# One tile per round in written order between two layers, self rows by plain transfers, and one bias folded into another

## The chip, the cores and the metric

The kernel runs on one NeuronCore of one Trainium2 chip, as a single program. Five engines each take their own instructions strictly in order: PE (matrix products and transposes), DVE (vector work), ACT (activations, and a queue of transfers of its own), POOL (a general processor that here mostly issues indexed transfers, called gathers) and SP (which only issues transfers). They wait for each other through semaphores. The metric is the device time of one execution in microseconds, the median of several runs; lower is better. Before the change it is 4209.92 us (three runs, 4207.29 to 4214.46).

## The reference, cut to what matters

The program is a stack of four blocks over a graph of 1250 nodes with 512 features. Each block adds a graph network, an attention and a feed-forward part to the residual x. Only the end of block 2 and the attention half of block 3 are touched:

```python
# end of block 2's feed-forward (z = residual + y + sh)
mu = jnp.mean(z, axis=-1, keepdims=True)
var = jnp.mean(jnp.square(z - mu), axis=-1, keepdims=True)
y2 = (z - mu) * jax.lax.rsqrt(var + 1e-05) * ln_g + ln_b
x = x + y2
# block 3
xn = _layernorm(x, axis=-1)
# graph convolution: every node also has an edge to itself, of weight 1
row_f = jnp.concatenate([row, loop]); col_f = jnp.concatenate([col, loop])
norm = dinv[row_f] * ew * dinv[col_f]
h = xn @ W
gnn = segment_sum(h[row_f] * norm[:, None], col_f) + b
# linear attention, phi(t) = elu(t) + 1, 8 heads of 64
q, k, v = split(xn @ w_qkv.T); q = phi(q * 0.125); k = phi(k)
mix = (q @ (k.T @ v)) / (q . sum(k) + 1e-8) @ w_out.T + b_out
x = x + gnn + mix
x = x + ffn3(_layernorm(x))          # 32 experts, 2 per token
```

## The kernel before, in words

Tiles and names. The 1250 nodes are ten tiles of 128 rows (the last has 98). x, z, xn hold all ten in on-chip memory; xnT is xn transposed. A product of one tile with a 512x512 matrix is `nat` (L196): four matmuls of 128x512, which the profile shows as eight records.

The end of block 2, called the tail here. `layer2_ffn` leaves four functions per tile in `self.tail` (L3252). `fetch` (L3229) issues two gathers on POOL, of the tile's two expert outputs; six buffers of the tile `g` rotate. `add_rows` (L3234) adds them to z (two DVE instructions, L3237) and takes z's mean and inverse deviation: bn_stats, bn_aggr and an add on DVE (L245 to L247), logarithm and exponential on ACT (L248, L249). `scale` (L3241) makes a bias on DVE (L3242), normalizes on ACT (L3245) and multiplies by gamma on POOL (L3246). `add` adds z to x on DVE (L214) and takes the statistics of x.

`tail_steps` (L2723) chains these four, then `norm` (L2726: xn, on DVE, L262) and `turn` (L2729: four transposes on PE, L2732, and a copy on ACT, L2734). It staggers them over rounds: in the round of tile t each later function works on a later tile. Before, `add` and `norm` of one tile are one step (`arrive`), so a tile passes five steps. `layer3_attn` calls the round of tile t with `need(t)`. In round 0, `load` also asks for the three attention matrices of 1 MB each, on SP, each behind a tiny fill on POOL (L169) that holds the load until then.

The first product of block 3. After each `need(t)` the tile is multiplied with the convolution's matrix (`nat`, L200), scaled on ACT into `o` (L3300) and written to the table gcn_h in device memory from ACT's queue (L3301). All gathers of block 3 read gcn_h, so the first of them waits for the tenth write.

The stage after it. The edges lie in 188 tiles of 128, 16 to a block of 107 target nodes (12 blocks, the last of 12 tiles). In each full block the sixteenth tile holds only the self edges: its 128 places are four runs of 32, of which 27 (26 in the last) are used. For an edge tile, `fetch` (L3317) gathers 128 rows of gcn_h into `hs` (POOL, L271; eight buffers, asked for six tiles ahead), `split` (L3322) makes a high part on ACT (L3326), a low part (L3327) and a one-hot matrix (L3330) on DVE, and PE adds two matmuls into the block's sum (L3366). At a block's end DVE scales and adds a bias (L3373), ACT's queue writes the block, and `add` (L3336) later reads finished rows back from SP (L3338) and adds them to x. Between groups of four edge tiles one step of the attention runs (`next(steps)`): the generator `linear_attention_steps` (L904) has ten steps of k products, ten that add up k and v (L950), one that makes the combined matrix, and then the q products and outputs. For each tile's output it first adds the attention's bias row to x on POOL (L979).

What sets the order. A scheduler orders each engine's instructions from the traced program by its own estimates, and may put an instruction of a later step ahead of one of an earlier step, as long as no data dependence forbids it. In the rounds of the tail only POOL keeps its text order before the change (L2747). `written_order` (L148) is a helper that chains all instructions traced inside it, engine by engine, so that each of the five engines keeps the text's order. Between the edge stage and the experts of block 3 SP also loads expert matrices (L3406) in the same queue as the read-backs.

Of the kernel before, what the change touches and what calls it, by code (L numbers as in the profile page):

```python
# [12 lines left out]
F32 = mybir.dt.float32  # L13
# [7 lines left out]
AF = mybir.ActivationFunctionType  # L21
ALU = mybir.AluOpType
# [3 lines left out]
D = 512  # L26
NT = 10
# [8 lines left out]
BN = 107  # L36
NB = 12
CB = 8
GE = 4
# [10 lines left out]
QN = 27  # L50
QK = 3
QC = 2 * QK
QP = 32
# [13 lines left out]
class Net:  # L67
# [79 lines left out]
    @contextmanager  # L147
    def written_order(self):  # L148

        traced = self.nc.cur_bb.bb.instructions  # L150
        last = traced[-1]
        yield
        at = next(k for k in reversed(range(len(traced))) if traced[k] is last) + 1
        queues = {e: None for e in (mybir.EngineType.PE, mybir.EngineType.DVE,
                                    mybir.EngineType.Activation, mybir.EngineType.Pool,
                                    mybir.EngineType.SP)}
        how = mybir.DependencyInfo(mybir.DependencyClass.NoSync, mybir.DependencyReason.DATA)
        for i in traced[at:]:
            if i.engine in queues:
                if queues[i.engine] is not None:  # L160
                    self.tc.add_manual_dep(i, queues[i.engine].name, how,
                                           reason="written_order")
                queues[i.engine] = i

    def weight(self, src, k, n, behind=False):

# [737 lines left out]
    def linear_attention_steps(self, xn, xT, w_qkv, w_out, b_out, qscale, finish, added=None,  # L904
                               need=None, ws=None):
# [4 lines left out]
        nc = self.nc  # L910
# [9 lines left out]
        with self.tc.tile_pool(name="la", bufs=1) as p, \  # L920
# [3 lines left out]
                wv = self.weight(w_qkv[:, 2 * D:3 * D], 4, D)  # L924
            else:
                wk, wv, wq = ws
            bo = self.rowvec(b_out)

            P = p.tile([128, 4, D], F32, name="P")
            ks = p.tile([128, D], F32, name="ks")  # L930
            for half in range(2):
# [12 lines left out]
                for c in range(5):  # L944
                    m = self.mm()
                    for i in range(HT):
                        t = half * HT + i
                        r = rows(t)
# [3 lines left out]
                    o = P[:, c, :] if c < 4 else ks  # L952
# [23 lines left out]
            for i in range(NT + 2):  # L976
                if i < NT:
                    r = rows(i)
                    nc.gpsimd.tensor_tensor(self.x[:r, i, :], self.x[:r, i, :], bo[:r],  # L979
                                            op=ALU.add)  # L980
                    q = tmp.tile([128, D], F32, tag="q", name="q")
                    phi(q, self.nat(xT, wq, i))
                    prod = tmp.tile([128, D], F32, tag="r", name="prod")
                    nc.vector.tensor_tensor(prod, q, ks, op=ALU.mult)
                    den = tmp.tile([128, 8], F32, tag="den", name="den")
                    nc.vector.tensor_reduce(den, prod.rearrange("p (h d) -> p h d", h=8), AX.X,
                                            ALU.add)
                    finish(den, den)
                    nc.vector.reciprocal(den, den)
                    q8 = q.rearrange("p (h d) -> p h d", h=8)  # L990
                    nc.vector.tensor_tensor(q8, q8, den.unsqueeze(2).to_broadcast([128, 8, 64]),
                                            op=ALU.mult)
                    Q[i] = q
                if 1 <= i <= NT:
                    qT = tmp.tile([128, 4, 128], F32, tag="qT", name="qT")
                    self.transpose_tile(qT, Q.pop(i - 1))
                    QT[i - 1] = qT
                yield
                if i >= 2:
                    t = i - 2  # L1000
                    self.add_to_x(t, self.nat(QT.pop(t), kvo, 0))
                    if added is not None:
                        added(t)
                    yield
# [1715 lines left out]
        self.tails = ExitStack()  # L2720
        return self.tails.enter_context(self.tc.tile_pool(name=name, bufs=1, side="right"))

    def tail_steps(self, xn, xnT, behind=None):  # L2723


        def norm(t):  # L2726
# [9 lines left out]
        tail = self.tail  # L2736
# [3 lines left out]
            last[0](t)  # L2740
            norm(t)

        steps = tail[:-1] + [arrive, turn]
        n = len(steps) - 1

        def need(t):
# [266 lines left out]
    def layer2_ffn(self):  # L3013
        nc, I = self.nc, self.I
        keep = self.begin_tail("l2t")
        self.begin_convs()
        with self.tc.tile_pool(name="l2f", bufs=1) as p:
            z = keep.tile([128, NT, D], F32, name="z")
            ga = keep.tile([128, D], F32, name="ga")
# [3 lines left out]
            with ExitStack() as es:  # L3023
# [48 lines left out]
                with self.tc.tile_pool(name="l2x", bufs=1) as px:  # L3072
# [3 lines left out]
                    for t in range(NT):  # L3076
                        self.norm_tile(t, z[:, t, :])
                        q = self.tp([128, 4, 128])
# [4 lines left out]
                        for i, (a, b, op) in enumerate(((0, 2, ALU.subtract), (0, 1, ALU.add),  # L3083
                                                        (1, 0, ALU.subtract))):
                            q = t * 128
# [137 lines left out]
            self.convs.close()  # L3223
        self.act_tables()
        mv = keep.tile([128, NT, 2], F32, name="mv")
        rs = keep.tile([128, NT, 2], F32, name="rs")
        pg = self.tails.enter_context(self.tc.tile_pool(name="l2g", bufs=6, side="right"))
        gs = {}

# [9 lines left out]
            self.row_stats(z[:, t, :], mv[:, t, :], rs[:, t, 0:1])  # L3239

        def scale(t):  # L3241
            nc.vector.scalar_tensor_tensor(rs[:, t, 1:2], mv[:, t, 0:1], -1.0, rs[:, t, 0:1],  # L3242
                                           op0=ALU.mult, op1=ALU.mult)
            c = z[:, t, :]
            nc.scalar.activation(c, c, AF.Identity, scale=rs[:, t, 0:1], bias=rs[:, t, 1:2])  # L3245
            nc.gpsimd.tensor_tensor(c, c, ga, op=ALU.mult)  # L3246

        def add(t):
            self.add_to_x(t, z[:, t, :])
            self.ready(t)  # L3250

        self.tail = [fetch, add_rows, scale, add]  # L3252
# [25 lines left out]
    def layer3_attn(self):  # L3278
        nc, I = self.nc, self.I
        added = self.both_added()  # L3280
        with self.tc.tile_pool(name="l3", bufs=1) as p:
# [4 lines left out]
            def load():  # L3286
                ws.extend(self.weight(I["L3_mix_w_qkvT"][:, i:i + D], 4, D, behind=True)
                          for i in (D, 2 * D, 0))

            need = self.tail_steps(xn, xnT, load)  # L3290
            th = self.dram.tile([NP, D], F32, name="gcn_h")
            H = self.dram.tile([NP, D], F32, name="gcn_sum")
            dinv = self.dinv
            w = self.weight(I["L3_gnn_W"], 4, D)
            keep = self.tails.enter_context(
                self.tc.tile_pool(name="gcn0", bufs=2, side="right"))
            for t in range(NT):
                need(t)
                o = keep.tile([128, D], F32, tag="o", name="o")
                nc.scalar.activation(o, self.nat(xnT, w, t), AF.Copy, scale=dinv[:, t:t + 1])  # L3300
                nc.scalar.dma_start(th[t * 128:(t + 1) * 128, :], o)  # L3301
            self.tails.close()
            with self.tc.tile_pool(name="gcn", bufs=2) as tmp:
                if self.fast:
                    dinvb = self.dinvb
                    bias = self.rowvec(I["L3_gnn_b"])
                else:
                    acc = tmp.tile([128, D], F32, tag="acc", name="acc", bufs=3)
                    nc.vector.memset(acc, 0.0)
                steps = self.linear_attention_steps(  # L3310
                    xn, xnT, I["L3_mix_w_qkvT"], I["L3_mix_w_outT"], I["L3_mix_b_out"], 0.125,
                    lambda o, d: nc.vector.tensor_scalar(o, d, 1e-8, None, op0=ALU.add),
                    added, ws=ws)

# [1 line left out]

                def fetch(t):  # L3317
                    hs = tmp.tile([128, D], F32, tag="hs", name="hs", bufs=8)
                    self.gather(hs, th[:, :], self.srcI[:, t:t + 1])
                    W[t] = hs  # L3320

                def split(t):  # L3322
# [21 lines left out]

                tiles = list(range(NT))
                T = self.groups * GE
                for t in range(6):
                    fetch(t)
                split(0)
                for g in range(self.groups):  # L3350
                    next(steps, None)
                    k = g % 4
                    last = not self.fast or k == 3 or g + 1 == self.groups
                    if not self.fast:
# [289 lines left out]
```

## Time and profile before

| what | value |
|---|---|
| median of three runs | 4209.92 us (4207.29 to 4214.46) |
| the profiled execution | 4223.65 us, of which the span of the trace is 4221.9 us |
| granted TensorE clock, mean | 0.939 |
| busy: PE, DVE, ACT, POOL | 87%, 60%, 33%, 29% |
| last expert output of block 2 written | 3481.41 us |
| first product of the tail starts / last table write issued | 3504.87 / 3564.22 us |
| first and last gather of the edge stage | 3571.04 / 3853.46 us |
| last block's bias and scale (L3373) | 3860.42 us |
| experts of block 3 and the end | 3887 to 4222 us |

How to read it. A window row gives, for one stretch of the span, each engine's busy time and number of instructions, then the granted clock of PE (1.00 is full), the share of the sixteen transfer engines that was busy, and GB/s. A wait row says which engine's line waited for whom: total us, times, longest. In the timeline a row is start, duration, engine, line and what it reads and writes; in square brackets stands the idle time before it and what ended it.

### The profile page before, as it was taken

What the parts mean: (1) busy time and instruction counts of PE and PEld (TensorE: products, weight loads), DVE (VectorE), ACT (ScalarE), POOL (GpSimd) and SP (SyncE); (2) the same over time, 40 slices, a digit from 0 to 9 for tenths busy, and PEclk for the clock granted to TensorE, in tenths of its full rate; (3) what the DMA queues carried; (4) which work ended last, traced back from release to release, by engine and by line L of the source; (5) the groups of instructions that cost most, each with busy time, mean ns of one, the idle gap of its engine ahead of it and who ended that gap; (6) DMA issues with size and microseconds to landing.
All of it is one profiled execution on the core that took longest, in us unless ns stands there. A gap on an engine that the chain in (4) does not pass through costs nothing. (4 is left out here: it accounts for less than half of the span.)

```text
span 4221.9 us, 48964 instructions
## 1 busy us (share of the span) xinstructions
PE 3680.2 (87%) x15172; PEld 2163.7 (51%) x15190; DVE 2546.1 (60%) x6105; ACT 1400.3 (33%) x2960; POOL 1204.3 (29%) x1229
## 2 busy tenths in 40 slices
PE   4996998899887669989999999979979986996898
PEld 2443443344333254447888776545456652554465
DVE  7556995885886835248966685142763335796311
ACT  2111332332224832105644462122532323553111
POOL 1007654663761030020000002030311015774422
PEclk9998999999998889999999999999989998996799
DMA  5718886985984154043211113660014654765796
GB/s 186 262 31 249 252 234 203 264 256 170 276 234 140 37 169 138 0 116 108 77 39 52 37 31 120 239 229 19 16 43 153 216 171 144 206 200 195 240 307 172
DMA packets 315682, 657.51 MB, mean 156 GB/s; under 512 B 78797, under 2 KB 128569, under 8 KB 300005
## 3 DMA queue, kind: packets, MB, share of 16 engines
q1 hardware_dynamic: 204909, 386.38, 28.5%
q0 software_dynamic: 73936, 227.19, 19.5%
q10 hardware_dynamic: 36568, 40.73, 2.8%
q8 instruction: 124, 2.03, 0.2%
q14 instruction: 145, 1.19, 0.1%
HBM read 532.93 MB, written 126.53 MB: 156 GB/s over the span
## 5 line engine op out<-in xcount | busy, mean ns | idle before, releaser
L271 POOL DMA_INDIRECT xl<-xl,srcI x531 | 547.5, 1031 | 347.3 <-issue 121.2
L1530 PE MATMUL mm<-hl,oh 118*128 118x512 f32 x564 | 341.3, 622 | 66.9 <-DVE s L1543 32.2
L2475 PE MATMUL more<-hh,e 128*128 128x259 f32 x1600 | 383.7, 385 | 9.2 <-ACT o L2418 8.2
L2475 PEld LDWEIGHTS more<-hh,e 128*128 128x128 f32 x1600 | 295.1, 191 | 72.2 <-issue 16.0
L200 PE MATMUL mm<-w,xnT 128*128 128x512 f32 x640 | 304.2, 615 | 15.0 <-ACT xnT L2734 12.9
L1533 PE MATMUL mm<-xl,ident 128*128 128x512 f32 x524 | 285.2, 626 | 21.6 <-DMA xl<-xl,srcI 21.4
L271 POOL DMA_INDIRECT hs<-gcn_h,srcI x188 | 213.8, 1137 | 81.7 <-issue 25.0
L1543 DVE TENSOR_TENSOR s<-xl,mm 128x512 f32<-128x512 f32 x302 | 205.8, 681 | 28.3 <-PE mm L1530 19.9
L1640 PE MATMUL more<-xl,wT 128*32 128x512 f32 x1698 | 212.7, 609 | 4.2 <-ACT wT L1621 4.2
L1530 PEld LDWEIGHTS mm<-hl,oh 118*128 118x128 f32 x564 | 107.0, 196 | 212.7 <-DVE s L1543 69.7
L1546 DVE SCALAR_TENSOR_TENSOR junk<-s,att 128x512 f32<-128x512 f32 x302 | 209.4, 693 | 10.6
L1546 DVE SCALAR_TENSOR_TENSOR junk<-mm,att 128x512 f32<-128x512 f32 x262 | 180.2, 688 | 57.4 <-PE mm L1533 46.3
L2395 ACT ACTIVATE e<-r,hh 128x512 f32<-128x512 f32 (+1 forms) x240 | 154.3, 646 | 137.2 <-PE more L2475 126.3
L200 PEld LDWEIGHTS mm<-w,xnT 128*128 128x128 f32 x640 | 122.1, 197 | 142.4 <-issue 118.2
L1506 ACT CAST oh<-nb 108x512 fp32r<-108x512 uint8 x141 | 86.8, 617 | 306.7 <-DMA nb<-nbt 292.0
L3366 PE MATMUL more<-hl,oh 128*128 128x512 f32 x376 | 152.9, 512 | 26.0 <-DVE oh L3330 11.3
L2398 ACT ACTIVATE e<-r,a 128x512 f32<-128x512 f32 (+1 forms) x240 | 152.4, 646 | 67.2 <-DVE e L2400 55.0
L2400 DVE TENSOR_TENSOR e<-e,e 128x512 f32<-128x512 f32 (+1 forms) x240 | 141.9, 597 | 50.9 <-ACT e L2395 46.8
L2338 PE MATMUL mm<-w,xnT 128*128 128x258 f32 x640 | 159.7, 392 | 7.4 <-DVE junk L2322 6.0
L881 PE MATMUL more<-ohs,ohb 128*128 128x512 bf16 (+1 forms) x546 | 132.6, 375 | 35.4 <-ACT ohs L865 14.8
L3326 ACT ACTIVATE hl<-hs,rec 128x512 fp32r<-128x512 f32 x188 | 130.7, 718 | 98.1 <-PE more L3366 52.1
L3327 DVE SCALAR_TENSOR_TENSOR hl<-hs,rec,hl 128x512 fp32r<-128x512 f32 x188 | 142.7, 771 | 24.9 <-ACT hl L3326 24.0
(674 smaller groups left out, 7273.6 us busy)
## 6 DMA issues: line engine op xcount, KB each, us to landing
w<-L_ffn_Wp SPq DMA_DIRECT2D x64, 1024.0 KB
w<-L_ffn_table SPq DMA_DIRECT2D x56, 1025.0 KB
neg<-ntab SPq DMA_DIRECT2D x80, 320.0 KB
hl<-xr SPq DMA_DIRECT2D x216, 108.0 KB
xr<-tro SPq DMA_DIRECT2D x30, 512.0 KB
xe<-routed_in SPq DMA_DIRECT2D x56, 256.0 KB
routed_out<-o ACTq DMA_DIRECT2D x56, 256.0 KB
c<-x SPq DMA_DIRECT2D x141, 64.0 KB
```

The lines of the kernel that those rows point to most:

```text
L200: self.nc.tensor.matmul(p, lhsT=xT[:, c, t * 128:(t + 1) * 128], rhs=w[:, c, n0:n0 + n], start=c == 0, stop=c == k - 1)
L271: self.nc.gpsimd.indirect_dma_start(out=out, out_offset=None, in_=table, in_offset=bass.IndirectOffsetOnAxis(ap=idx, axis=0), bounds_check ...
L1530: nc.tensor.matmul(m, lhsT=s, rhs=rows_pair(b, pair)[:K], start=not last, stop=not on_pe(i))
L1533: nc.tensor.matmul(m, lhsT=self.ident, rhs=d["xl"][:, j, :D], start=False, stop=True)
L1543: nc.vector.tensor_tensor(o, d["xl"][:, j, :D], s, op=ALU.add)
L1546: nc.vector.scalar_tensor_tensor(junk, s, 0.0, L["att"], op0=ALU.max, op1=ALU.mult, accum_out=B[g // 4]["lg"][:, i % 16:i % 16 + 1])
L1640: nc.tensor.matmul(d["y"][ps], lhsT=d["w", i][:, ps], rhs=rows_of(t), start=i == 0, stop=False)
L2338: nc.tensor.matmul(m, lhsT=chunk(layer, c)[:, t * 128:(t + 1) * 128], rhs=w[:, c, :], start=c == 0, stop=c == k - 1)
L2395: nc.scalar.activation(e1[:, :n], R[q, k, 0][:, :n], AF.Exp, bias=HH[q][:, s, 256:257])
L2398: nc.scalar.activation(e2[:, :n], R[q, k, 1][:, :n], AF.Exp, bias=heads[q][0][:, s, 0:1])
L2475: nc.tensor.matmul(ys[j], lhsT=e[:, j * 128:(j + 1) * 128], rhs=HH[q][:, s, :], start=s == 0, stop=s == NT - 1)
L3366: nc.tensor.matmul(y, lhsT=oh, rhs=hl[:, i], start=i + j == 0 and not (self.fast and k), stop=last and i + j == GE)
```

## The change

It has three parts. In the tail, `scale` becomes one DVE instruction, (z - mean) * gamma, and the inverse deviation is applied where z is added to x (`add_scaled`, one DVE instruction); the ACT and POOL passes and the small DVE bias are gone. `arrive` is split into `add` and `norm`, so a tile passes six steps, and the whole loop over `need`, product and table write is put into `written_order`, with the table write of tile t - 1 placed between the round of tile t and its product. For the first twelve groups of the edge stage, everything traced on PE, DVE and ACT is ordered behind the last instruction of that engine that was traced before the stage.

In the edge stage, the sixteenth tile of the blocks 0 to 10 is fetched by four plain transfers of 32 consecutive rows each from SP instead of one gather on POOL (eleven tiles of 188).

The attention's bias row is added once to the convolution's bias row on DVE, and the ten additions of it to x on POOL are gone.

```diff
+    def last_of(self, engine):
+        return next(i for i in reversed(self.nc.cur_bb.bb.instructions) if i.engine == engine)
+
+    def after(self, first, others):
+        how = mybir.DependencyInfo(mybir.DependencyClass.NoSync, mybir.DependencyReason.DATA)
+        for i in others:
+            if i.engine == first.engine:
+                self.tc.add_manual_dep(i, first.name, how, reason="after")
...
-            bo = self.rowvec(b_out)
+            bo = None if b_out is None else self.rowvec(b_out)
...
-                    nc.gpsimd.tensor_tensor(self.x[:r, i, :], self.x[:r, i, :], bo[:r],
-                                            op=ALU.add)
+                    if bo is not None:
+                        nc.gpsimd.tensor_tensor(self.x[:r, i, :], self.x[:r, i, :], bo[:r],
+                                                op=ALU.add)
...
-    def tail_steps(self, xn, xnT, behind=None):
+    def tail_steps(self, xn, xnT, behind=None, apart=False):
...
-        steps = tail[:-1] + [arrive, turn]
+        steps = tail + [norm, turn] if apart else tail[:-1] + [arrive, turn]
...
         def scale(t):
-            nc.vector.scalar_tensor_tensor(rs[:, t, 1:2], mv[:, t, 0:1], -1.0, rs[:, t, 0:1],
-                                           op0=ALU.mult, op1=ALU.mult)
             c = z[:, t, :]
-            nc.scalar.activation(c, c, AF.Identity, scale=rs[:, t, 0:1], bias=rs[:, t, 1:2])
-            nc.gpsimd.tensor_tensor(c, c, ga, op=ALU.mult)
+            nc.vector.scalar_tensor_tensor(c, c, mv[:, t, 0:1], ga, op0=ALU.subtract,
+                                           op1=ALU.mult)
 
         def add(t):
-            self.add_to_x(t, z[:, t, :])
+            self.add_scaled(t, z[:, t, :], rs[:, t, :])
             self.ready(t)
...
-            need = self.tail_steps(xn, xnT, load)
+            need = self.tail_steps(xn, xnT, load, True)
...
-            for t in range(NT):
-                need(t)
-                o = keep.tile([128, D], F32, tag="o", name="o")
-                nc.scalar.activation(o, self.nat(xnT, w, t), AF.Copy, scale=dinv[:, t:t + 1])
-                nc.scalar.dma_start(th[t * 128:(t + 1) * 128, :], o)
+            with self.written_order():
+                def put(t, y):
+                    o = keep.tile([128, D], F32, tag="o", name="o")
+                    nc.scalar.activation(o, y, AF.Copy, scale=dinv[:, t:t + 1])
+                    nc.scalar.dma_start(th[t * 128:(t + 1) * 128, :], o)
+
+                y = None
+                for t in range(NT):
+                    need(t)
+                    if y is not None:
+                        put(t - 1, y)
+                    y = self.nat(xnT, w, t)
+                put(NT - 1, y)
...
+                    mixed = self.rowvec(I["L3_mix_b_out"])
+                    nc.vector.tensor_tensor(bias, bias, mixed, op=ALU.add)
...
-                    self.gather(hs, th[:, :], self.srcI[:, t:t + 1])
+                    b, k = divmod(t, 4 * GE)
+                    if self.fast and k == 4 * GE - 1 and b < NB - 1:
+                        for q in range(4):
+                            r = b * BN + QN * q
+                            nc.sync.dma_start(hs[QP * q:QP * q + QP, :], th[r:r + QP, :])
+                    else:
+                        self.gather(hs, th[:, :], self.srcI[:, t:t + 1])
...
+                traced = nc.cur_bb.bb.instructions
+                ahead = [self.last_of(e) for e in (mybir.EngineType.PE, mybir.EngineType.DVE,
+                                                   mybir.EngineType.Activation)]
+                n0 = len(traced)
                 for t in range(6):
                     fetch(t)
                 split(0)
                 for g in range(self.groups):
                     next(steps, None)
+                    if g < 12:
+                        for i in ahead:
+                            self.after(i, traced[n0:])
+                        n0 = len(traced)
```

More of the change, by code (lines that the diff above doesn't have):

```diff
@@ L3225, in layer2_ffn @@
         mv = keep.tile([128, NT, 2], F32, name="mv")
-        rs = keep.tile([128, NT, 2], F32, name="rs")
+        rs = keep.tile([128, NT, 1], F32, name="rs")
         pg = self.tails.enter_context(self.tc.tile_pool(name="l2g", bufs=6, side="right"))
@@ L3310, in layer3_attn @@
                 steps = self.linear_attention_steps(
-                    xn, xnT, I["L3_mix_w_qkvT"], I["L3_mix_w_outT"], I["L3_mix_b_out"], 0.125,
+                    xn, xnT, I["L3_mix_w_qkvT"], I["L3_mix_w_outT"],
+                    None if self.fast else I["L3_mix_b_out"], 0.125,
                     lambda o, d: nc.vector.tensor_scalar(o, d, 1e-8, None, op0=ALU.add),
```

## The prediction

> **What bounds the kernel now.** I read the page's costliest groups first, then windows over the touched stretch, then the waits of its parts, then the timeline between the last products of the tail and the first gather.
>
> The windows (stretch, then busy us and instructions of PE, weight loads, DVE, ACT, POOL, then granted clock, transfer share, GB/s):
>
> ```profile
> 3481.00:3503.00 22.00, 0.00 (x0) 0.00 (x0) 11.09 (x30) 5.03 (x12) 12.59 (x11) 0.58 0.37 109
> 3503.00:3571.00 68.00, 53.01 (x136) 24.18 (x136) 38.69 (x86) 24.26 (x62) 29.82 (x28) 0.91 0.43 147
> 3571.00:3600.00 29.00, 21.97 (x57) 11.32 (x58) 19.33 (x38) 16.91 (x26) 22.56 (x22) 0.88 0.67 186
> 3600.00:3800.00 200.00, 196.74 (x616) 107.88 (x615) 174.21 (x371) 110.56 (x182) 155.03 (x135) 1.00 0.70 203
> 3800.00:3862.00 62.00, 45.09 (x114) 21.44 (x112) 50.00 (x111) 29.24 (x45) 42.94 (x40) 0.81 0.67 203
> ```
>
> Three regimes are to be seen: a tail (3481 to 3571) in which no engine is full; a middle (3600 to 3800) in which PE is busy 196.7 of 200 us; and an end (from 3800) in which PE idles 17 us of 62. The page's row of the gathers (busy us, mean ns, idle before them):
>
> ```profile
> L271 POOL DMA_INDIRECT hs<-gcn_h,srcI x188 | 213.8, 1137 | 81.7 <-issue 25.0
> ```
>
> And the longest wait from 3800 to 3862 (total us, times, longest):
>
> ```profile
> ACT hl L3326 <- DMA hs<-gcn_h,srcI: 17.9, 18, 3.2
> ```
>
> From 3620 to 3800 that same wait is 6.0 us in 5 times; in the end it is 17.9 us. The end is paced by gathers: POOL issues them back to back, 1.0 us and more each plus 0.3 between, and its waits there are nearly all that 0.3.
>
> The timeline of the tail's last tile:
>
> ```profile
> 3550.31 0.55 DVE L262 TENSOR_SCALAR xn<-x,mvx,rsx 128x512 f32<-128x512 f32 x1 [0.50 <-ACT rsx L249]
> ...
> 3558.35 0.60 PE L2732 MATMUL tp<-ident,xn 128*128 128x128 f32 x4
> ...
> 3559.14 0.58 ACT L2734 COPY xnT<-tp 128x512 f32<-128x512 f32 x1
> ...
> 3559.77 10.57 PE L200 MATMUL mm<-w,xnT 128*128 128x512 f32 x24 [0.82 <-ACT xnT L2734]
> ...
> 3564.22 0.33 ACTq L3301 DMA_DIRECT2D gcn_h<-o  x1
> ```
>
> DVE has normalized the last tile at 3550.9, but its transposes stand behind two other products and start at 3558.35. The 24 records are tile 9's product and two k products of the attention. The last table write leaves at 3564.22, the first gather starts 6.8 us later, at 3571.04.
>
> **The change: the order.** In the built programs everything before the tail stands in the same order, but for the new addition of the two bias rows; from the first edge tile on, PE, DVE and ACT keep their orders instruction for instruction. So holding the attention's first steps back changes nothing after the tail, and within it PE still does ten first products and then two k products. New are the order in the tail and the queues of POOL and SP.
>
> **The change: the tail.** What counts is when the last write leaves (3564.22 before). ACT loses ten L3245 (0.81 us), POOL ten L3246 (1.33 us) and five L979 (1.27 us); DVE loses ten tiny L3242, and gains ten passes of 0.75 us (as L3237). In text order a round's vector work for one tile, from start to start in dependent order, is 2 x 0.78 (L3237) + 0.72 + 0.22 + 0.06 (statistics) + 0.67 (scale) + 0.78 (add) + 1.00 (statistics) + 0.47 (norm) = 5.5 us. PE's round is 0.79 (transposes to copy) + 0.63 (copy to product) + 3.56 (eight records of 0.445) = 5.0 us. Round 0 must first run five `add_rows`, four `scale`, three `add`, two `norm`. With the landings seen before (3488.27, then about 1.4 apart) the last of these `add`s ends at 3510.5; ACT's copy stands behind its statistics, so the first product starts at 3511.8, 7 us later than before (3504.87). It takes 5.5 us, as before. Then come 5.5 us rounds while `add_rows` lasts, and 5.0 us rounds: product 9 starts at 3559.0, and the write leaves at 3563.4. With DVE 6% slower it is 3566.2, with 12% 3569; if product 1 is also slow (6.23 us before, at a clock of 0.53) 3565.4. I take 3564.8, nearer the clean rows since POOL's passes, which stretched L3237 to 2.11 us, are gone: **+0.6 us**, ends -0.8 and +5. POOL's twenty gathers of the tail (1.14 us each) stay ahead of DVE: the ninth and tenth are asked for by 3498 and used from 3506. The three attention weights are asked for after twelve gathers instead of ten, at about 3498.5 instead of 3506.1, still long before the k products. The wait of ACT's activation of wq (1.91 us, L936) moves behind the last write and lies in the 5.96 us in which ACT waited for that write. The bias addition (0.69 us, DVE) lies in the experts, where DVE waits for PE over 1 us at a time; if it doesn't, +0.7.
>
> **The change: self rows and bias on POOL.** POOL loses 11 of 188 gathers and five L979 in the edge stage (1.28 us each). Worth by regime:
> At the start tile t's gather is 1.31 us behind its forerunner; without tile 15's the later ones come 1.3 us earlier, and ACT waits for them (11.8 us from 3575 to 3620): **-1.3**.
> In the middle POOL isn't the limit: its gain only builds up a lead. Two L979 (3710.19 and 3747.10) fall where DVE is 95 to 100% busy; the L3327 beside the first took 1.62 instead of 0.75: 2 x 0.9 = **-1.8**, ends 0 and -2.6.
> At the end POOL's lead decides. Counting back from the last gather (tile 187, 3853.46), POOL issues tile 162 at 3817.59, when DVE splits tile 158 (3817.94). Eight buffers allow 166. In the middle POOL saves 9 x 1.44 + 4 x 1.44 = 19 us, so it will stand at that limit: four tiles. Tile 175 is a plain transfer: a fifth. 25 intervals take 35.87 us, 1.435 each: 5 x 1.435 = **-7.2**. DVE would allow more: 28 tiles at 0.87 and 5.9 us of other passes end at 3848, 11 us before tile 187's pair, so DVE isn't reached. Ends: 0 (transfers, not POOL, pace it) and -11.
>
> SP now issues 44 transfers of 64 KB more, in order with the read-backs and expert loads. No row shows such a transfer; 0.35 us an issue makes 1.4 us a tile, and landing as the gathers' (3.5 to 4.7 us from issue). The tightest is tile 159: behind the read-back at 3806.43, it would land at 3812.4, and ACT takes the tile near 3816.6. Slack 4 us: 0 taken, upper end +4 at each of blocks 9 and 10.
>
> Past the last block (3860.42) nothing differs: routing and experts move along.
>
> At this point the Trainium skill speaks against the change ("DMA: Bandwidth & Descriptors", Issuing engines are not separate DMA queues): all queues run on the same sixteen engines, so a second issuer saves only issue time. By that alone the -7.2 would be 0 if the engines paced the end. The rows: transfer share 0.67 there, but 1.04 at 401 GB/s from 3515 to 3520, and POOL issuing without a pause; issue time is the thing short here.
>
> **Sum.** +0.6 - 1.3 - 1.8 - 7.2 = -9.7 us. The profiled execution took 4223.65 (span 4221.9 and 1.75 around it), 13.7 above the median of 4209.92; a fresh one would take 4213.9, and the median 4200.2: 0.23% less.
>
> **Rivals.**
> *Transfers pace the end.* For: 4.2 to 4.7 us from issue to ACT at the end against 3.5 at the start. Against: the share of 0.67. Then only +0.6 - 3.1: 4207.4.
> *POOL paces every block.* For: sixteen gathers at 1.137 + 0.34 are 23.6 us, and blocks take 22.5 to 25.0 (one 30.8). Against: PE 196.7 of 200. Then 11 x 1.48 + 5 x 1.44 = 23.5 goes: 4187.
> *The one-tile rounds leave PE cold, and it is slower.* PE pauses twice in each round. If the clock stays near 0.5, each product takes 6.23 instead of 3.56 us: nine times 2.67 is 24, against the 10.3 won: 4224. It decides where pauses are as long as the 5.07 us ahead of product 1. Against: from 3525 to 3560 PE was busy 28.4 of 35 us, with pauses up to 2.1, at clock 1.00; the rounds now have 4.16 of 5.5 and pauses of 1.3. The Trainium skill ("TensorE: Matmul & The Clock Gate", The HAM clock gate) needs an idle window of about 3.4 us for the slow clock; by it this rival falls.
> *SP brings self rows late.* Each late one holds ACT, and with it PE; 4 us at two blocks: 4208. Against: the slack above.
>
> **How the numbers follow.** Mine 0.46, transfers 0.19, every block 0.18, cold 0.08, SP 0.09. The measurement tells about 0.2%, 8.4 us: faster means under 4201.5, slower over 4218.3. Mine alone reaches from 4195 to 4206, and 0.65 of it is faster: 0.30, with every block 0.48, and 0.01 of the rest. Slower: cold, and 0.01 more. The range takes in 4188 (all 22 us of PE's idle time after the first 5 are won) and 4212 (tail +5, only -3.1 won). Cases of both signs hold most of the chance, so mine stands beside it: 4195 to 4206.
>
> **What would show it.** Right: first product near 3512, rounds of 5 to 5.5 us at clock 1.00, last write within 3 us of 3564; blocks up to the eighth as long as before within 1 us; ACT's wait for hs after 3800 well under 10 us; last block's bias about 10 us earlier against the same start. Wrong: products of 6 us; PE idle before the sixteenth tiles; SP's read-backs behind a self row; an end that still advances 1.4 us a tile with POOL idle.

## The result and the profile after

The changed kernel takes 4191.1 us (median of five, 4185.3 to 4194.0) against 4210.8 (five, 4207.3 to 4220.6) for the kernel before: a ratio of 0.9948, interval 0.9934 to 0.9962. That is faster by 0.52%, or 19.7 us; I had forecast 4200, 9.7 us less. Direction and range held, the size is twice the forecast, and the measured time lies below the 4195 to 4206 that I had given for my own mechanism alone. The first question is whether the other 10 us belong to the change.

The profiled execution of after took 4188.4 us (span 4186.2). Its windows over the answering stretches (us, then busy us and instructions of PE, weight loads, DVE, ACT, POOL, then granted clock, transfer share, GB/s):

```profile
3465.00:3487.00 22.00, 0.00 (x0) 0.00 (x0) 14.41 (x32) 3.31 (x11) 14.87 (x16) 0.58 0.52 146
3487.00:3553.00 66.00, 50.77 (x136) 23.43 (x136) 39.25 (x84) 20.20 (x53) 10.11 (x7) 0.91 0.39 139
3553.00:3582.00 29.00, 21.12 (x57) 10.76 (x57) 18.81 (x37) 16.55 (x26) 22.46 (x22) 0.94 0.67 188
3582.00:3778.00 196.00, 195.91 (x617) 108.12 (x616) 169.25 (x372) 109.72 (x182) 142.81 (x125) 1.00 0.71 210
3778.00:3836.50 58.50, 44.73 (x112) 22.09 (x111) 49.44 (x110) 29.28 (x45) 40.85 (x34) 0.74 0.67 206
```

The tail is no fuller than before. In the middle PE is now busy 195.9 of 196 us: the 3.3 us that it idled there are gone. The end is shorter, but PE still idles 14 us in it, now at a mean clock of 0.74 instead of 0.81. POOL has 11 gathers fewer, each no faster (page, costliest groups):

```profile
L282 POOL DMA_INDIRECT hs<-gcn_h,srcI x177 | 205.8, 1163 | 118.3 <-ACT r L927 48.7
```

The waits of the end, from 3778 to 3837 (total us, times, longest), against 17.9 and 4.6 us before:

```profile
ACT hl L3353 <- DMA hs<-gcn_h,srcI: 11.4, 11, 2.0
...
ACT hl L3353 <- PE more L3401: 10.0, 11, 1.8
```

The tail's last tile, in the timeline of after:

```profile
3529.06 0.55 DVE L273 TENSOR_SCALAR xn<-x,mvx,rsx 128x512 f32<-128x512 f32 x1 [1.60 <-ACT rsx L260]
...
3540.81 0.60 PE L2744 MATMUL tp<-ident,xn 128*128 128x128 f32 x4
3541.45 0.58 ACT L2746 COPY xnT<-tp 128x512 f32<-128x512 f32 x1 [3.64 <-PE tp L2744]
...
3542.08 10.57 PE L211 MATMUL mm<-w,xnT 128*128 128x512 f32 x24 [0.68 <-ACT xnT L2746]
...
3546.54 0.33 ACTq L3311 DMA_DIRECT2D gcn_h<-o  x1
...
3553.14 1.00 POOL L282 DMA_INDIRECT hs<-gcn_h,srcI  x1 [48.70 <-ACT r L927]
```

The last tile waits 11 us for PE, the last write leaves at 3546.54, and POOL, without work for 48.7 us, gathers first at 3553.14.

These clock times are all earlier than before, but not by the change alone: the load of the first product's weight, which SP asks for ahead of the tail, left at 3476.07 before and at 3459.79 after. The profiled execution of before (4223.65 us) lies 13 us above its median, that of after 3 us below its own. So the two executions are compared by stretches, cut at the same instruction in both (starts in the timelines, us; "router" runs from the last block's bias to the first routed write):

| stretch | before | after | difference | forecast |
|---|---|---|---|---|
| start of the kernel to that weight load | 3476.1 | 3459.8 | -16.3 | 0 |
| to the last table write | 88.15 | 86.75 | -1.4 | +0.6 |
| to the first gather | 6.82 | 6.60 | -0.2 | 0 |
| to block 0's bias | 27.14 | 27.42 | +0.3 | -1.3 |
| to block 8's bias | 200.00 | 195.60 | -4.4 | -1.8 |
| to block 11's bias | 62.24 | 59.21 | -3.0 | -7.2 |
| router | 46.65 | 39.73 | -6.9 | 0 |
| experts, to the end | 314.80 | 311.09 | -3.7 | 0 |

What the change touches gives -8.7 us, near my -9.7, made up of other terms. The other 27 us lie in code in which PE, DVE, ACT, POOL and SP keep their orders (but for one DVE addition). The experiments ask which of them come back.

### The profile page after: what moved, and what is told of

Its sections match the earlier page's. It is cut to its first block, busy times and chain, and to the rows that moved or that the text cites. A ratio compares the mean times of both kernels' runs of the same rounds, so it can differ in the third digit from the quotient of the medians.

```text
span 4186.2 us, 48993 instructions
## 1 busy us (share of the span) xinstructions
PE 3667.5 (88%) x15172; PEld 2155.6 (51%) x15190; DVE 2544.6 (61%) x6106; ACT 1393.6 (33%) x2950; POOL 1172.6 (28%) x1198
## 5 line engine op out<-in xcount | busy, mean ns | idle before, releaser
L211 PE MATMUL mm<-w,xnT 128*128 128x512 f32 x640 | 301.3, 609 | 15.8 <-ACT xnT L2746 13.7
L282 POOL DMA_INDIRECT hs<-gcn_h,srcI x177 | 205.8, 1163 | 118.3 <-ACT r L927 48.7
L1518 ACT CAST oh<-nb 108x512 fp32r<-108x512 uint8 x141 | 86.9, 618 | 324.4 <-DMA nb<-nbt 302.4
L3600 DVE TENSOR_SCALAR o<-mm,d 98x512 f32<-98x512 f32 x32 | 24.0, 750 | 216.2 <-PE mm L3597 102.2
```

The source lines that it names most:

```text
L211: self.nc.tensor.matmul(p, lhsT=xT[:, c, t * 128:(t + 1) * 128], rhs=w[:, c, n0:n0 + n], start=c == 0, stop=c == k - 1)
L282: self.nc.gpsimd.indirect_dma_start(out=out, out_offset=None, in_=table, in_offset=bass.IndirectOffsetOnAxis(ap=idx, axis=0), bounds_check ...
```

## Experiment 1: both kernels once more, and the change in three parts

The runs from here on were made in three later series, each beside the kernel before. In the first two, layer 0's edge layers are some 160 to 260 us slower (median of before: 4473 and 4406 us) and single times of before spread over 46 to 71 us. Whether the chip makes this difference is not shown: the first and the third of them ran on a chip of the same number, 10, and before took 4473 us in one and 4405 us in the other. So medians are compared within one series only, and the stretches behind layer 0 across series with care. First both kernels again, unchanged.

> The kernel before, once more, for a second trace. In the first two traces the stretch from the last block's bias to the first routed write took 46.65 us before and 39.73 us after, with the same instructions: the granted clock was 0.50 through the router's products before, and rose to 1.00 in the middle of them after. If that state belongs to the kernel, this trace shows 46.5 to 46.8 us and clock 0.50 from the last block to the first routed write again. If it is chance (the clock changes in steps of 3.41 us, wherever these fall), it may be anywhere from 38 to 47 us here. The 16 us by which the trace of before was late already ahead of the tail should not come back: tail's first write near 3460, time near 4210.

> The changed kernel once more, for a second trace and as the base of the next three. If the plain transfers carry the gain and nothing else is systematic, the parts of the trace are as in the first one: last table write 86.7 us after the load of the first product's weight is asked for, last three blocks 59.2 us (62.2 to 62.8 without plain transfers), and the routing either 39.8 or 46.7 to 47.3 us by chance. Time: 9 us under before by the sum of these parts, 20 us under it if what the first comparison showed beyond them is real.

The totals of another series tell nothing of the 16 us ahead of the tail. But the router took 39.81 us in the kernel before, and 47.25 in the changed one: each other's length of the first pair. The windows of the router in the first traces of before and after:

```profile
3860.50:3907.00 46.50, 27.35 (x124) 25.04 (x124) 26.07 (x71) 4.11 (x10) 0.00 (x0) 0.53 0.42 168
```

```profile
3835.40:3875.00 39.60, 20.59 (x124) 18.34 (x124) 26.19 (x69) 4.10 (x10) 0.00 (x0) 0.63 0.50 198
```

And in the second traces of before and after:

```profile
4129.40:4169.10 39.70, 20.56 (x124) 18.34 (x124) 26.23 (x70) 4.10 (x10) 0.00 (x0) 0.63 0.50 197
```

```profile
4047.40:4094.50 47.10, 28.45 (x124) 26.12 (x124) 26.18 (x69) 4.11 (x10) 0.00 (x0) 0.50 0.42 166
```

The same 124 products take 20.6 us where the clock rises on the way and 27.4 to 28.5 where it does not. So the 6.9 us of the first pair are chance, not the change. Among the ten traces here whose router stands in this order, four are short (39.7 to 39.8) and six long (46.7 to 47.3).

Then the parts. The tail alone, which is the changed kernel with these lines back as before:

```diff
-                    b, k = divmod(t, 4 * GE)
-                    if self.fast and k == 4 * GE - 1 and b < NB - 1:
...
-                    else:
-                        self.gather(hs, th[:, :], self.srcI[:, t:t + 1])
+                    self.gather(hs, th[:, :], self.srcI[:, t:t + 1])
...
-                    mixed = self.rowvec(I["L3_mix_b_out"])
-                    nc.vector.tensor_tensor(bias, bias, mixed, op=ALU.add)
...
-                    xn, xnT, I["L3_mix_w_qkvT"], I["L3_mix_w_outT"],
-                    None if self.fast else I["L3_mix_b_out"], 0.125,
+                    xn, xnT, I["L3_mix_w_qkvT"], I["L3_mix_w_outT"], I["L3_mix_b_out"], 0.125,
```

> Before, with the tail of the change alone (written order, one tile per round, the new scale, the first steps held back); all 188 gathers, and the second bias on POOL. My sum: +0.6 us, time within 2 us of before (4211). If the tail itself were the gain, -10 us or more. By the two traces -1.5 us from the last table write on. The first product 7 us later than in before against the same first landing, rounds 4.8 us without transfers at the end; blocks and end as in before.

The plain transfers alone (the kernel before, with these lines):

```diff
+                    b, k = divmod(t, 4 * GE)
+                    if self.fast and k == 4 * GE - 1 and b < NB - 1:
+                        for q in range(4):
+                            r = b * BN + QN * q
+                            nc.sync.dma_start(hs[QP * q:QP * q + QP, :], th[r:r + QP, :])
+                    else:
+                        self.gather(hs, th[:, :], self.srcI[:, t:t + 1])
-                    self.gather(hs, th[:, :], self.srcI[:, t:t + 1])
```

> Before, with the plain transfers of eleven own tiles alone. My sum: -8.5 us (start -1.3, end -7.2): 4202. By the traces, the edge stage from first gather to last block bias was 289.4 us before and 282.2 after; if the plain transfers carry it, it is 282 to 284 here and the time 4204 to 4206. If the routing's clock belongs to how the end is left, another -6.8 us: 4197 to 4199. If transfers pace the end, 4207 or more.

The bias alone:

```diff
-            bo = self.rowvec(b_out)
+            bo = None if b_out is None else self.rowvec(b_out)
...
+                    if bo is not None:
+                        nc.gpsimd.tensor_tensor(self.x[:r, i, :], self.x[:r, i, :], bo[:r],
+                                                op=ALU.add)
...
+                    mixed = self.rowvec(I["L3_mix_b_out"])
+                    nc.vector.tensor_tensor(bias, bias, mixed, op=ALU.add)
...
+                    None if self.fast else I["L3_mix_b_out"], 0.125,
```

> Before, with the two bias rows added once (ten POOL additions go, one DVE addition comes). My sum: -1.8 us (two additions beside a full DVE), 4209. If POOL's additions cost nothing, 4211. If POOL paced every block, ten additions of 1.28 us plus 0.16 each: -14 us. In the trace: the two blocks with passes of hl stretched to 1.62 us become 0.9 us shorter each, the others unchanged.

Ratios to the kernel before, with intervals, and stretches (us; weight load to last write, first gather to block 0's bias, and on from there):

| kernel | ratio | to last write | to block 0 | to block 8 | to block 11 | router | experts |
|---|---|---|---|---|---|---|---|
| before again | - | 88.22 | 33.83 | 203.44 | 62.84 | 39.81 | 316.62 |
| tail alone | 0.9997 (0.9968 to 1.0026) | 87.90 | 33.35 | 209.09 | 62.81 | 47.27 | 315.51 |
| plain transfers alone | 0.9954 (0.9933 to 0.9976) | 88.12 | 31.30 | 200.76 | 59.82 | 47.33 | 311.99 |
| bias alone | 0.9978 (0.9953 to 1.0002) | 85.70 | 33.89 | 205.62 | 63.99 | 39.82 | 312.86 |
| after again (its own series) | 0.9956 (0.9928 to 0.9984) | 86.81 | 32.74 | 196.07 | 60.46 | 47.25 | 309.33 |

The plain transfers carry it: the only part whose interval leaves out 1, and the end falls by 3.0 us, exactly as in the whole change. The edge stage takes 291.9 us with them against 300.1 in the kernel before of the same series, 8.2 less; the 282 to 284 us that I expected were not met, as the stage is longer in both kernels here. The tail alone changes the total by -1.0 us, within its interval. Its own stretch is 0.3 us shorter than before (87.90 against 88.22), with passes of `add_rows` stretched beside a bias addition that POOL still makes there (timeline of the tail alone):

```profile
3784.17 2.43 DVE L3249 SCALAR_TENSOR_TENSOR z<-g,ev,z 128x512 f32<-128x512 f32 x2
...
3784.35 1.71 POOL L991 TENSOR_TENSOR x<-x,b 128x512 f32<-128x512 f32 x1 [12.45 <-DVE xn L273]
```

The six pairs of these passes before it take 1.53 to 1.54 us.

The bias gives its price where I had looked for it: the two blocks with stretched passes go from 33.73 and 25.64 to 29.87 and 24.35 us here, and from 30.78 and 25.64 to 29.88 and 24.46 in the first pair, 2.1 us together there (forecast 1.8). In its trace other blocks, which I had expected unchanged, were longer (block 1 by 2.2, block 3 by 3.8 us), so that its total, -10 us with 0 inside the interval, can't be read from that one execution.

## Experiment 2: layer 0's edge layers left out

To rid the totals of layer 0's spread, four kernels were run without its three edge layers, so that what they compute differs from the program; from layer 1 on, the first three have the orders of the full kernels.

```diff
-            for k in range(3):
-                otab = self.dram.tile([NP, D], F32, name="x%d" % (k + 1))
...
+            for t in range(NT):
+                self.ready(t)
```

> The kernel before without layer 0's three edge layers (they are left out, x goes on without them). From layer 1 on the order is that of before on every engine. In the traces so far the same code of these layers took from 250 us less to 16 us less in one execution than in another, and the rest of the program repeated within a few us; without them the spread of single times should fall from 30 to 70 us to under 15 us, and the medians of this and the next three can be compared with each other to about 3 us. Their ratio to the full kernel before says nothing.

> The changed kernel, cut in the same way. Against the short kernel before: my sum says -9.7 us; the parts of the traces say -8.6 us (tail -1.4, edge stage -7.2), or -12 to -13 if the 4 us by which the experts were shorter wherever plain transfers were used belong to the change; if the medians of the full kernels (-19.7 and -16 us) are right, -16 to -20. Routing's two lengths (39.8 and 47 us) are chance in all of these theories and spread single times by 7 us.

> The kernel before with the plain transfers alone, cut in the same way. My sum: -8.5 us against the short kernel before, 1.2 us behind the changed one. By the traces -6 to -8 us (blocks to the eighth -2.7, last three -3.0, start 0 to -2.5), so the tail and the bias together are worth 1.5 to 4 us more in the changed one. If the full kernels' -19.6 is right, -16 to -20, and the same as the changed kernel.

Medians (range), us: before 3213.3 (3207.7 to 3229.3), changed 3201.9 (3190.7 to 3207.1), plain transfers alone 3203.6 (3200.8 to 3212.2). The spread fell to 11 to 22 us, not under 15 for all; the router's two lengths can make 7 of it. The changed kernel is 11.3 us faster by the medians, and no time of one lies among those of the other; the plain transfers alone give 9.7. The medians are near my sums (9.7 and 8.5). But the means differ by 17.3 us (3216.5 and 3199.2) and by 12.0 for the transfers alone, so that five to seven times that spread by 11 to 22 us can't tell 10 us from 20. One profiled execution of each in this series, which was one of the slowest of before (3229.0) and the fastest of the changed kernel (3190.7):

| stretch | before | transfers alone | changed |
|---|---|---|---|
| to last write | 88.00 | 88.07 | 86.59 |
| first gather to block 0 | 34.80 | 31.64 | 32.55 |
| to block 8 | 204.73 | 199.28 | 196.31 |
| to block 11 | 64.56 | 60.24 | 59.40 |
| router | 47.32 | 47.32 | 39.74 |
| experts | 315.58 | 312.40 | 313.10 |

The edge stage gains 15.8 us here against 7.2 in the first pair. In the four later traces without plain transfers it takes 300.1 to 305.3 us, in the first one 289.4; with them 286.0 to 293.0 in eight later traces and 282.2 in the first. So what the relief of POOL is worth is not one number here. Whether the chip or something else makes the stage longer in the kernels without it is open.

One thing stays open: the experts. Without plain transfers they took 312.9 to 316.6 us (five traces, mean 315.1), with them 308.2 to 314.4 (nine traces, those of experiment 3 included, mean 311.5). The orders there are the same in all fourteen. The two ranges overlap, and four of the nine come from the second series, in which no kernel without transfers was profiled. I have no mechanism for the 3.5 us of the means, and nothing was tried on them.

## Experiment 3: what sets the end now

I had expected -7.2 us at the end, and it gave -3.0. Two causes are possible: POOL's lead is smaller than I took it for, or PE's half clock has become the limit, since ACT now waits 10.0 us for PE (4.6 before; 5.3 in the second trace of after). First, twelve buffers instead of eight:

```diff
-                    hs = tmp.tile([128, D], F32, tag="hs", name="hs", bufs=8)
+                    hs = tmp.tile([128, D], F32, tag="hs", name="hs", bufs=12)
```

> The changed kernel with twelve hs buffers instead of eight. In the trace of after POOL last stood still for a buffer at tile 151 (it waited for the split of tile 143), then issued 1.41 us apart while ACT took tiles 1.2 us apart, so that its lead was used up by tile 166 and ACT waited for gathers again. If that lead sets the end, four tiles more are worth up to 4 x 1.41 = 5.7 us: last three blocks 53.5 to 56 us instead of 59.2, ACT's wait for hs there under 4 us instead of 11.4. If PE's half clock sets the end (0.50 in 34 of the last 60 us), the last three blocks stay within 1 us of 59.2 and ACT waits for PE instead.

The last three blocks took 55.47 us instead of 60.46 (after again, same series): -5.0, of 5.7 at most; against the other two traces of the changed kernel (59.21 and 59.40) it is -3.7 to -3.9. Windows over exactly these blocks, after again:

```profile
3986.90:4047.30 60.40, 45.41 (x117) 21.84 (x115) 49.79 (x110) 30.71 (x47) 43.57 (x35) 0.79 0.69 208
```

and with twelve buffers:

```profile
4009.80:4065.30 55.50, 43.35 (x117) 21.43 (x115) 49.45 (x111) 30.52 (x47) 38.82 (x33) 0.85 0.71 213
```

and ACT's wait for gathers in them, 13.0 us in after again,

```profile
ACT hl L3353 <- DMA hs<-gcn_h,srcI: 13.0, 14, 2.0
```

is halved with twelve, though not under the 4 us that I expected:

```profile
ACT hl L3353 <- DMA hs<-gcn_h,srcI: 6.2, 6, 1.9
```

So the lead sets the end in the main, at a transfer share that hardly moved (0.69, 0.71). How it is used up is seen when gathers and splits are counted in the timeline. In the first trace of after, POOL's issues around tiles 150 and 151, and at tile 162:

```profile
3773.77 1.47 POOL L282 DMA_INDIRECT hs<-gcn_h,srcI  x1 [0.39 <-DVE oh L3357]
...
3776.33 1.03 POOL L282 DMA_INDIRECT hs<-gcn_h,srcI  x1 [0.73 <-DVE oh L3357]
...
3791.74 1.08 POOL L282 DMA_INDIRECT hs<-gcn_h,srcI  x1 [0.30 <-issue]
```

From tile 151 on POOL never pauses for more than its 0.3 us. Tile 151 was asked for 1.3 us after its buffer came free, tile 162 2.1 us after, tile 170 4.3 us after: from tile 151 to 162 POOL needs 1.40 us a tile, while DVE takes one every 1.2 us. At tile 162 the gather starts 7.2 us ahead of the low part of its split; before it was 5.2. That is 2.0 us of lead won, where I had counted four tiles, 5.7 us. With twelve buffers tile 151 is 15.1 us ahead, tile 162 12.0, tile 170 7.9, and ACT waits again from tile 174.

As a whole, twelve buffers were no gain over before, ratio 1.0007 (0.9977 to 1.0038), and by the medians they lost that of the change: 4413.7 us against 4390.2 in the same series. From the first gather to block 0 the trace shows 39.81 us instead of 32.74, and the router, whose order the scheduler changed, 49.41 instead of 47.25; together with the shorter end, that places about 4 of the 23.6 us. Why the first block is longer was not tried; ACT waits 10.5 us for gathers there instead of 5.6, the granted clock is 0.70 instead of 0.84, and PE, DVE and ACT all have idle times of 2 to 4 us, some of them waiting for nothing that the profile shows.

Then the clock: one more product a tile in the last three blocks, zero times hl, to keep PE's clock up, with eight buffers and with twelve:

```diff
+                zero = tmp.tile([128, 128], F32R, name="zero", bufs=1)
+                nc.vector.tensor_scalar(zero, self.iota, -1.0, None, op0=ALU.is_equal)
...
+                        if self.fast and g >= 36 and not (last and j == GE - 1):
+                            for _ in range(1):
+                                nc.tensor.matmul(y, lhsT=zero, rhs=hl[:, 0], start=False,
+                                                 stop=False)
```

> The changed kernel, with one more product a tile in the last three blocks (PE adds zero times hl to the block's sum, 0.35 us at full clock), to keep PE's clock up; eight buffers. If the half clock sets the end, the last three blocks take 54 to 57 us instead of 59.2. If POOL's lead sets it, they stay at 59 us within 1, and only the clock differs: 1.00 instead of 0.74 there. The routing, if PE enters it at full clock and keeps it: 33 to 37 us; if the clock falls at its narrow products whatever came before: 39.8 to 47.3.

> Twelve buffers and the extra products together. If both limits bind in turn, the last three blocks take 50 to 54 us, less than in either alone. If the lead alone sets the end, the same as with twelve buffers alone; if the clock alone, the same as with the extra products alone.

With eight buffers the last three blocks took 58.14 us, 2.3 less than after again and 1.1 less than the first trace of after, at a clock of 0.91:

```profile
3997.70:4055.90 58.20, 50.11 (x158) 28.50 (x156) 50.28 (x112) 30.94 (x47) 42.17 (x35) 0.91 0.72 216
```

```profile
ACT hl L3355 <- DMA hs<-gcn_h,srcI: 10.7, 12, 2.1
```

ACT still waits 10.7 us for gathers. With both edits the blocks took 56.83 us, not less than with twelve buffers alone (55.47); the "both bind in turn" of 50 to 54 failed. By these single traces the half clock is worth 1 to 2 us at the end, the lead 4 to 5. Ratios: 0.9959 (0.9934 to 0.9984) with the product alone, level with the changed kernel; 1.0004 (0.9977 to 1.0031) with both.

> The changed kernel with the extra product a tile in the last three blocks, cut in the same way. By the trace of the full one: last three blocks 58.1 us instead of 59.2 to 60.5, routing 37.8 us instead of 39.8 or 47.3: -2 to -10 us against the short changed kernel, about -5 in the median. If routing's clock is chance here too, half of the executions have 44 us and more there, and the gain is under 2 us.

In the short form the product alone gave 3193.7 us (3187.8 to 3197.4), 8.2 less than the short changed kernel, though the ranges overlap; last three blocks 57.57, router 37.73 (37.76 in the full one, in neither of the ranges expected). In the form without layer 0's edge layers it has the lowest median; in the full form its median is 5.6 us above that of the changed kernel (4395.7 and 4390.2), within the spread. Since the scheduler also changed the router's order in it, whether the clock or the order gives 37.7 is not settled.

## Why the prediction was right, and where it was not

Right: faster, inside the range, for the reason given (POOL's relief, not the tail). The touched stretches give -8.7 us against -9.7. But all four terms were off and made up for each other, so that the closeness of the sum is luck. Two signs that I had named for being right did not come either: ACT's wait for gathers at the end was 11.4 us, not well under 10, and blocks 3 and 6 became 2.0 and 1.2 us shorter, where I had every block up to the eighth the same within 1. The terms:

- *Tail, +0.6.* It gave -1.4 (the changed kernel and its variants 86.6 to 86.9 in seven traces; the old tail 88.0 to 88.2 in five; the new tail with the bias additions still on POOL 87.9; the old tail without them 85.7, the shortest of all). So the new tail by itself is worth 0.3 us at most by these traces, and most of the -1.4 goes with the bias additions. The working held: moved by the 16.3 us of the start, I had the first product at 3495.5 and it came at 3495.37; rounds of DVE 5.5 and 5.49; PE's 5.0 and 4.81; product 9 at 3542.7 and 3542.08. The failing step is "I take 3564.8": the clean estimate (3563.4) was the better value, since no pass of `add_rows` was stretched once POOL's work was gone (all 0.74 to 0.75 us).
- *Start, -1.3.* +0.3 in the first pair; -2.2 in the short kernels, -2.5 with the plain transfers alone against before in the same series. Why the first pair shows no gain here is open.
- *Middle, -1.8.* The bias gave 2.1 us, near what I counted (the second stretched pass, at 3746.93, took 2.02 us, more than the 1.62 that I had doubled). The failing step is "In the middle POOL isn't the limit: its gain only builds up a lead". ACT's wait for gathers between block 0's and block 8's bias, before:

```profile
ACT hl L3326 <- DMA hs<-gcn_h,srcI: 10.2, 11, 2.5
```

and after:

```profile
ACT hl L3353 <- DMA hs<-gcn_h,srcI: 1.3, 2, 1.0
```

PE's idle time there went with it. I had quoted 6.0 us of this wait and charged nothing for it. Block 3 alone became 2.0 us shorter (25.02 to 23.02); in it ACT had waited 5.6 us for gathers, and now waits 0.3.

- *End, -7.2.* -3.0. The failing step is "it will stand at that limit: four tiles". POOL is close to the buffers' limit only up to tile 151, and eleven tiles later the lead has shrunk to 1.4 tiles more than before. Twelve buffers brought 4 to 5 us more, so the mechanism (the end is paced by POOL, from the lead it enters with) stands.
- *Past the last block "nothing differs: routing and experts move along".* For the router that is right but for chance (7 us). For the experts, 3.5 us in the mean stay unexplained.
- *The other 11 us of the median difference of the first pair* are not placed. Its interval (0.9934 to 0.9962, that is -28 to -16 us) leaves out -9.7. Router and layer 0 vary by 7 us and more between executions, but that this shifted the medians is not shown, and the short kernels (11.3 us by medians, 17.3 by means) do not settle it.

The rivals: transfers do not pace the end, or more buffers could not have given 4 to 5 us. Taking transfers off POOL's queue gave 3.0 us there, because POOL's time to issue was the thing short. The Trainium skill ("DMA: Bandwidth & Descriptors", Issuing engines are not separate DMA queues) says that a second issuing engine saves only the time to initiate a transfer, and that this is usually small; here it set the pace, with 1.16 us a gather and 0.3 us between two. POOL does not pace every block: four of the eight blocks before the end changed by 0.2 us or less. The tail's rounds did not leave PE cold: the clock is 1.00 from 3499 to 3557, with pauses of 0.7 to 1.4 us. This agrees with the Trainium skill ("TensorE: Matmul & The Clock Gate", The HAM clock gate), by which the slow clock follows an idle window of about 3.4 us. SP brought no own tile late at the end: tile 159's four transfers left from 3786.49 and ACT took it at 3793.02 without a pause, tile 175's from 3805.66 and at 3815.09; the four issues of a tile took 1.7 us, not the 1.4 of my estimate.

## What to carry to other kernels

An engine that is relieved early helps a later stretch only by the lead that it can carry there: find the last place at which it really stands still for a buffer, and run both paces on from that place, instead of multiplying the buffers by the interval. A wait that stands in the list of a stretch whose engine looks full is still worth what that engine idles there. And where code ahead of the change varies by more than the change is worth, cut it away or compare stretches between the same instructions, and count the spread that is left: here the cut-down kernels showed 11 us by their medians and 17 by their means, and the full ones 16 to 20.

## What the hardware showed that I had not expected

The router's 7 us. In the first trace of before, PE is recorded as busy without a break, at half clock, for 20 us (4 us windows):

```profile
3864.00:3868.00 4.00, 4.00 (x20) 4.00 (x21) 1.29 (x3) 0.13 (x1) 0.00 (x0) 0.50 0.20 66
...
3880.00:3884.00 4.00, 4.00 (x21) 4.00 (x21) 1.57 (x7) 0.41 (x2) 0.00 (x0) 0.50 1.00 418
```

In after, the clock rises during the same products:

```profile
3840.00:3844.00 4.00, 4.00 (x20) 4.00 (x21) 1.36 (x3) 0.51 (x1) 0.00 (x0) 0.51 0.15 57
3844.00:3848.00 4.00, 4.00 (x39) 4.00 (x38) 2.79 (x6) 0.66 (x2) 0.00 (x0) 1.00 0.00 0
```

Two thirds of these products are 32 columns wide, and weight loads fill PE beside them. So a PE that is busy by its records need not wake the clock. In both traces the clock holds each value for multiples of 3.41 us, apart from the ends of the trace. This agrees with the free-running window that the Trainium skill ("TensorE: Matmul & The Clock Gate", The HAM clock gate) describes. In after, the twelve 128-column products in a row (3841.51 to 3844.19) lie almost whole in the window that ends at 3843.94; in before, a window's edge at 3866.9 cuts them (3865.88 to 3868.68). All ten traces whose router stands in this order bear it out: in the four short ones 2.43 to 2.80 us of that row lie within one window, in the six long ones 1.53 to 2.35. That this decides it is an inference from ten traces, and nothing was changed to test it; that the same kernel comes out either way is shown.
